# Four graph layers on one Trainium2 core: layer 2's counts on four column tiles of TensorE, and layer 1's last eighth of sources in two pieces

## The chip, the cores and the metric

The kernel runs on one core of a Trainium2 chip. Time is microseconds (us) of device time per execution. The kernel before took 7437.63 us, the median of 10 runs (7422.31 to 7447.1). A profile shows one execution, with these engines: PE (TensorE) does matmuls and PEld its weight loads, DVE is VectorE, ACT is ScalarE, POOL is GpSimd, SP is SyncE, which here only issues DMAs. The granted clock is the share of full speed at which TensorE was allowed to run in a stretch.

## The reference

8192 nodes have 32 features each, and 262,144 edges are sorted by their destination. Four layers follow each other; each adds the sum of its messages to x and normalizes every node's row.

```
out0 = segment_sum(einsum(x[src], weight0[edge_type]), dst)     # 64 relations
out1 = segment_sum(x[src] * edge_weight[:, None], dst)
out2 = segment_sum(x[src], dst)
out3 = segment_sum(messages from x[src], an MLP of edge_attr_32, edge_attr_4, ...)
x = layernorm(x + out_l)                                        # after every layer
```

## The kernel before

A node block is 128 nodes (64 blocks); an edge block g is 1024 edges (256 blocks). All engines' orders are written out by hand in one function: an instruction waits only for the semaphore marks that are named ahead of it (`after`), and each engine works through its list in order. The DMAs of layers 1 and 2 are issued by SP in the order of the program.

**Layer 0** (L878 to L935) is a loop over g from 0 to 257. POOL gathers each edge's row of a table that the prologue (to about 230 us) has made (L454, eight gathers per block, twelve blocks ahead; the two halves of block g+12 wait for marks of PE in block g). DVE cuts the rows into three bf16 parts (L858 to L863) and makes one-hot pairs of the destinations (L583); PE sums eight tiles by destination (L897). Each four blocks the sums are moved out (L869), and as soon as all edges of 8 node blocks are summed, `windows` (L575, shifted sums on PE) and `normalize` (L525 to L537) finish an eighth of x_b, the input of layer 1.

**The matrices.** Blocks 8 to 207 also make 256 matrices of the edges (`matrices`): one-hots on DVE (L638 to L643), products on PE (L654), two evictions on ACT (L658 counts as bytes, L659 weighted sums), and on SP one store of the weighted part to famat (L664) and one of the counts to fcmat (L666). Layer 1 is then a dense product of famat with x_b, layer 2 of fcmat with x_a.

**Layer 1** has 32 destination pieces c (two node blocks each) by 8 source eighths z. One item (c, z) is 1 MB of famat, loaded by SP (L695), and 8 fp32 matmuls with 32 columns of weights (16 records at L717), which go to the four column tiles of PE in turn: four sources sum side by side on 4 x 32 partitions. `take` (ACT, L726) moves a run of items of one c out; `turn_back` (PE, L736) or `turn` (L980) adds the four groups by a matmul with a stack of identities; `add_up` (DVE, L752) adds the run to y1. `plan()` says which item runs in which block g: an item may run once its eighth is normalized and its matrix stored; 1.5 items are due per block, 3 from block 200 on, in at most two runs per block. Of the 256 items, 224 (z = 0 to 6) run in layer 0; the last of them go two per block up to block 245, and blocks 246 to 255 have none. The 32 items of z = 7 follow the last normalization in the *late part* (L990 to L1008): per piece one item, a take, a turn with two matmuls, and a normalization each four pieces. Three 1 MB slots hold items in the loop, six in the late part (`slot_of`). `acc_free` lets the products of a block wait for the adds of the block before.

**Layer 2** (L1013 to L1044) has 16 pieces c of 512 destinations. `bring` (SP, L783) loads 4 MB of counts into one of two buffers; it waits for the last cast of piece c - 2. `widen` casts bytes to bf16 in four ring parts, shared 48, 56 and 24 of 128 between DVE, ACT and POOL (L802, `SHARE`). PE then does 64 matmuls (L1033) with 96 columns of weights (x_a in three bf16 parts, side by side) and 512 of counts, into 96 partitions; ACT moves them out (L1039), `turn` adds the three parts, `normalize` follows each second piece, and SP stores the normalized rows to fxtab (L549).

**Layer 3**, from about 4341 us on, and its self parts (L961, L969) are not touched.

Of the kernel before, what the change touches and what calls it, by code (L numbers as in the profile page):

```python
# [21 lines left out]
P = 128  # L22
N = 8192
E = 262144
D = 32
# [44 lines left out]
RATE = lambda g: 1.5 if g < 200 else 3.0  # L70


def plan():

    normed, n = [], 0
    for g in range(GG):
        if g >= 2 and (g - 2) % 4 == 3:
            while n < NQ1 and ready(n) <= g - 1:
                n += 1
        normed.append(n)  # L80
    got = [0] * NC1
    out, job, due = [], None, 0.0
    for g in range(GG):
        r, m = normed[max(0, g - 1)], made_by(max(0, g - 4))
        due = min(due + RATE(g), 3)
        ended = 0
        while due >= 1:
            if job is None:
                room = NQ1 if ended == 0 else int(due) if ended == 1 else 0
                todo = [(min(r - got[c], room), -c) for c in range(NC1) if m >= 8 * (c + 1) and r > got[c]]  # L90
                if not todo or room == 0:
                    break
                k, c = max(todo)
                job = (-c, got[-c], got[-c] + k)
            c, z0, z1 = job
            z = got[c]
            out.append([g, c, z, z == z0, z + 1 == z1, ended])
            got[c] += 1
            due -= 1
            if z + 1 == z1:  # L100
                job = None
                ended += 1
    if job is not None:
        out[-1][4] = True
    return out
# [46 lines left out]
NQ1 = 8  # L152
# [9 lines left out]
def in_order(ctx: ExitStack, tc, x, a, w0, w1, b1, w2, si, keep):  # L162
# [11 lines left out]
    for k in range(2):  # L174
        m[f"amat{k}"] = dram.tile([NC1 // 2, NQ1, P * 2048 + 2304], FP, name=f"famat{k}")
# [28 lines left out]
def raw_layers(tc, x, a, w0, w1, b1, w2, si, m, bad):  # L204
# [8 lines left out]
    amat = [m["amat0"], m["amat1"]]  # L213
# [44 lines left out]
    st_a = cut(2, 8, 4 * 64).rearrange("p b z (q h w) -> p b z q h w", q=4, h=2)  # L258
# [256 lines left out]
    lnf, lns = m["lnf"], m["lns"]  # L515
# [3 lines left out]
    def normalize(l, c, acc, pm, x_in, x_out, x3=None, more=None):  # L519


        ds = slice(c * LC, (c + 1) * LC)
        y, yc, sq = (lnf[:, k].rearrange("p (d f) -> p d f", f=D) for k in range(3))
# [6 lines left out]
        vm = V.mark(V.e.tensor_sub(yc, y, lns[:, 1, :, None].to_broadcast([P, LC, D])))  # L530
# [6 lines left out]
        ln_last[0] = V.mark(V.e.tensor_tensor(xo, yc, lns[:, 3, :, None].to_broadcast([P, LC, D]), op=OP.mult))  # L537
# [14 lines left out]
    def windows(c, acc, free):  # L552

        d0 = c * LC
        todo = []
        for j in [0, 1, 2, 3, -2, -1, 4]:
            lo, hi = 0, LC
            while 4 * (d0 + lo) + j < 0:
                lo += 1
            while 4 * (d0 + hi - 1) + j >= GG:  # L560
                hi -= 1
            if lo < hi:
                todo.append((j, lo, hi))
# [67 lines left out]
    def matrices(i):  # L631
# [14 lines left out]
        for q in range(4):  # L646
# [4 lines left out]
            for j in range(4):  # L651
                for h in range(2):
# [8 lines left out]
                two[:, :, 256:512].rearrange("p h (z w) -> p h z w", w=32), AF.Copy))  # L661
# [3 lines left out]
                                   st_a[:, b].rearrange("p z q h w -> p z (q h w)")))  # L665
# [8 lines left out]
    m_ld = [Landing(tc, f"ld_m{k}") for k in range(8)]  # L674
    land1, used1, loaded = {}, {}, [0]
    acc_free = [None]
    sums1_free = [None, None]
# [4 lines left out]
    def slot_of(n):  # L682

        r = n - n_in
        if r < 0:
            return 3 + n % 3, n - 3
        order = [0, 1] + [3 + (n_in + k) % 3 for k in range(3)] + [2]
        return order[r % 6], n - 6 if r >= 6 else n - 5 if 2 <= r < 5 else None

    def load1(n, *more):  # L690

        c, z = items[n]
        k, before = slot_of(n)
        S.after(stored[8 * c + 6], stored[8 * c + 7], used1.get(before), *more)
        land1[n] = m_ld[k].add(S.e.dma_start(slot1[k], amat[c // 16][c % 16, z, 0:P * 2048].rearrange("(p w) -> p w", w=2048)))  # L695

    def pump():

        while loaded[0] < n_in + 5:
            n = loaded[0]  # L700
            c, z = items[n]
            before = slot_of(n)[1]
            if made < 8 * (c + 1) or (before is not None and before >= 0 and before not in used1):
                break
# [4 lines left out]
    def products(n, acc, first, last):  # L709

        c, z = items[n]
        k = slot_of(n)[0]
        PE.after(land1[n], normed[z])
        mv = slot1[k].rearrange("p (u h s j) -> p s u h j", h=2, s=8, j=4)
        for s in range(8):
            q = s % 4
            ins = PE.e.matmul(acc[q * D:(q + 1) * D, :].rearrange("p (u h j) -> p u h j", h=2, j=4),  # L717
                              x_b[:, 8 * z + s, :], mv[:, s], start=(first and s < 4), stop=(last and s >= 4),
# [10 lines left out]
    def turn_back():  # L729
# [4 lines left out]
        for c, h, k, am in todo:  # L734
            for d in range(2):
                ins = PE.e.matmul(bank[:, 6, 256 * h + d * D:256 * h + (d + 1) * D], sums1[:, k, d * P:(d + 1) * P], stack,  # L736
# [8 lines left out]
    def add_up():  # L745
# [3 lines left out]
        while added:  # L749
            c, h = added.pop(0)  # L750
            o, v = y1[:, 2 * c:2 * c + 2, :], bank[:, 6, 256 * h:256 * h + 2 * D].rearrange("p (d f) -> p d f", f=D)
# [5 lines left out]
    def layer1(g):  # L757

        ended = []
        while order1 and order1[0][0] == g:  # L760
            _, c, z, first, last, h = order1.pop(0)
            n = n_in - len(order1) - 1
            PE.after(acc_free[0])
            pm = products(n, bank[:, 6, 256 * h:256 * (h + 1)], first, last)
# [3 lines left out]
        for c, h in ended:  # L768
            turned.append((c, h, h, take(sums1[:, h], bank[:, 6, 256 * h:256 * (h + 1)], pm, sums1_free[h])))
# [17 lines left out]
    SHARE = (0, 48, 104, 128)  # L787
# [17 lines left out]
    def early_counts(g):  # L805

        k = g - soon[0]
        if k == 0:
            ring_free[0] = ring_free[1] = now(PE)
            for n in (n_in, n_in + 1):  # L810
# [67 lines left out]
    for g in range(GG + 2):  # L878
        if g >= 2 and (g - 2) % per == per - 1:
            vm = bank_out((g - 2) // per)  # L880
            while done < NB // LC and ready(done) <= g - 1:
                acc = bank[:, (g - 2) // per % 2, 0:LC * D]
                agg_free[(g - 2) // per % 2] = vm = normalize(0, done, acc, windows(done, acc, (vm,)), x_a, x_b)
# [49 lines left out]
    while loaded[0] < min(len(items), n_in + 6):  # L933
# [38 lines left out]
    def turn(l, c, n, am):  # L972

        nb = 2 if l == 1 else 4
        kk = 128 if l == 1 else 96
# [3 lines left out]
        for d in range(nb):  # L979
            ins = PE.e.matmul(bank[:, 2 + o, (d0 + d) * D:(d0 + d + 1) * D], sums[0:kk, n % 2, d * P:(d + 1) * P],  # L980
                              stack[0:kk, :], start=True, stop=True)
        sum_free[n % 2] = pm = PE.mark(ins)
        if d0 + nb == LC:
            out_free[o] = normalize(l, c * nb // LC, bank[:, 2 + o, 0:LC * D], pm, x_b if l == 1 else x_a,
# [8 lines left out]
    for c in range(NC1):  # L993
        b = c % 2
        PE.after(sum_bank[b])
        for e in range(got[c], NQ1):
            pm = products(n, bank[:, b, 0:256], e == got[c], e == NQ1 - 1)
            if n + 6 < len(items):
                load1(n + 6)
            n += 1  # L1000
        sum_bank[b] = am = take(sums[:, b, 0:256], bank[:, b, 0:256], pm, sum_free[b])
        if pend:
            turn(*pend)
        pend = (1, c, c, am)
        if c == 0:
# [8 lines left out]
    for c in range(16):  # L1014
# [14 lines left out]
        for k in range(4):  # L1029
            PE.after(*cast[c][k])  # L1030
            mv = ring[k].rearrange("p (u s j) -> p s u j", s=16, j=4)
            for s in range(16):
                ins = PE.e.matmul(bank[0:96, b, 0:512].rearrange("p (u j) -> p u j", j=4), x3[:, 16 * k + s, :], mv[:, s],  # L1033
                                  start=(k == 0 and s == 0), stop=(k == 3 and s == 15))
# [5 lines left out]
            sums[0:96, b, 0:512].rearrange("p (u j h) -> p u h j", h=2, j=4),  # L1040
            bank[0:96, b, 0:512].rearrange("p (u h j) -> p u h j", h=2, j=4), AF.Copy))
# [158 lines left out]
    for q in range(NQ + LAG3 + 2):  # L1200
# [73 lines left out]
        if 0 <= c < NQ and c % 2 == 1:  # L1274
# [9 lines left out]
            while done < NB // LC and ready(done) <= g + 1:  # L1284
                k, wp = w_bank()
                acc = bank[:, 3 + 2 * k, 0:LC * D]
                windows(done, acc, (w_free[k], gm))
                w_free[k] = normalize(3, done, acc, PE.mark(written(3 + 2 * k, 256)), z, x_a)
# [472 lines left out]
```

## Time and profile before

| stage (us of the span) | length | PE busy | DVE | ACT | POOL | clock | DMA share |
|---|---|---|---|---|---|---|---|
| prologue, 0 to 230 | 230.0 | 160.6 | 72.7 | 121.1 | 70.7 | 0.72 | 0.97 |
| layer 0 with matrices, to 3540 | 3310.0 | 1980.2 | 1893.7 | 1175.4 | 1683.6 | 0.68 to 0.78 | 0.38 to 0.63 |
| rest of layer 0, to 4011.8 | 471.8 | 193.2 | 157.6 | 33.4 | 269.0 | 0.58 | 0.44 |
| late part of layer 1, to 4096.3 | 84.5 | 72.1 | 38.9 | 23.2 | 4.4 | 0.68 | 0.91 |
| layer 2, to 4341.2 | 244.9 | 242.3 | 150.1 | 202.6 | 164.6 | 0.98 | 0.71 |
| layer 3, to 7438.2 | 3097.0 | 2417.6 | 2099.8 | 695.5 | 1937.8 | 0.89 | 0.11 |

The profiled execution took 7439.92 us; its span from the first to the last instruction is 7438.2. Columns of engines are busy us within the stage; records that run together count once. Windows of the trace give such rows for any stretch; timelines list instructions with their start, duration, engine, line, result and operands, and in brackets the idle time before them with what released them ("remote" where the profile knows no releaser). Records of one kind that follow each other are joined (x16 is sixteen records); an fp32 matmul shows as two records.

### The profile page before, as it was taken

What the parts mean: (1) busy time and instruction counts of PE and PEld (TensorE: products, weight loads), DVE (VectorE), ACT (ScalarE), POOL (GpSimd) and SP (SyncE); (2) the same over time, 40 slices, a digit from 0 to 9 for tenths busy, and PEclk for the clock granted to TensorE, in tenths of its full rate; (3) what the DMA queues carried; (4) which work ended last, traced back from release to release, by engine and by line L of the source; (5) the groups of instructions that cost most, each with busy time, mean ns of one, the idle gap of its engine ahead of it and who ended that gap; (6) DMA issues with size and microseconds to landing.
All of it is one profiled execution on the core that took longest, in us unless ns stands there. A gap on an engine that the chain in (4) does not pass through costs nothing.

```text
span 7438.2 us, 89563 instructions
## 1 busy us (share of the span) xinstructions
PE 5066.1 (68%) x34750; PEld 3346.2 (45%) x34750; DVE 4412.9 (59%) x9506; ACT 2251.0 (30%) x3323; POOL 4130.0 (56%) x4236
## 2 busy tenths in 40 slices
PE   7236666666666666666436977887877787877777
PEld 3125555555555555555223534444444444444444
DVE  3246565565566565555324646666666676676666
ACT  5223333333333333333101832222222222222222
POOL 3655555454454454444662666666666666666664
PEclk7557776777777777778556988898989888889988
DMA  9224444544645656667536721110111111111111
GB/s 356 89 57 143 128 140 139 177 145 162 206 155 189 208 187 209 208 214 248 198 113 237 278 88 25 24 25 21 25 24 25 24 24 25 24 25 24 25 24 18
DMA packets 583331, 865.52 MB, mean 116 GB/s; under 512 B 102640, under 2 KB 441840, under 8 KB 549360
## 3 DMA queue, kind: packets, MB, share of 16 engines
q1 hardware_dynamic: 448320, 782.88, 30.3%
q0 software_dynamic: 134144, 73.67, 5.2%
q8 instruction: 276, 4.52, 0.2%
q10 hardware_dynamic: 432, 3.15, 0.1%
q14 instruction: 159, 1.30, 0.1%
HBM read 454.48 MB, written 404.88 MB: 116 GB/s over the span
## 4 chain that ended last, share of the span: by engine, by line
PE 38%; another core or an unknown queue 24%; DVE 19%; ACT 10%; issue 8%; DMA 2%; POOL 1%; SPq 0%; DVEq 0%; ACTq 0%; POOLq 0%
PE bank L654 15%; PE bank L1221 7%; DVE f_arena L1256 4%; PE bank L1211 4%; ACT f_arena L659 3%; PE bank L1033 3%; ACT f_arena L658 3%; DVE f_arena L1252 3%; PE bank L717 2%; DVE f_arena L588 2%; DVE f_arena L1249 1%; ACT bank L1190 1%; PE bank L475 1%; PE bank L897 1%
## 5 line engine op out<-in xcount | busy, mean ns | idle before, releaser
L454 POOL DMA_INDIRECT f_arena<-fytab,f_row x2048 | 1955.3, 955 | 1802.6 <-PE bank L654 813.7
L454 POOL DMA_INDIRECT f_arena<-fxtab,f_src x2048 | 1937.8, 946 | 1112.5 <-issue 562.4
L654 PE MATMUL bank<-f_arena 64*128 64x128 f32 x16384 | 1514.7, 352 | 926.1 <-ACT f_arena L659 554.8
L654 PEld LDWEIGHTS bank<-f_arena 64*128 64x128 f32 x16384 | 1385.7, 257 | 1035.1 <-issue 541.8
L1221 PE MATMUL bank<-f_arena 128*128 128x344 f32 x4096 | 1495.9, 508 | 59.4 <-issue 58.6
L658 ACT ACTIVATE f_arena<-bank 128x512 uint8<-128x512 f32 x1024 | 613.1, 599 | 1796.4 <-remote 834.4
L1221 PEld LDWEIGHTS bank<-f_arena 128*128 128x128 f32 x4096 | 818.8, 211 | 642.4 <-issue 379.3
L1211 PE MATMUL bank<-f_arena 64*128 64x256 f32 x4096 | 660.5, 445 | 552.2 <-ACT bank L1190 456.7
L1190 ACT ACTIVATE bank<-f_arena 128x1024 f32<-128x1024 f32 x512 | 526.2, 1029 | 1118.2 <-DVE f_arena L1256 659.2
L1211 PEld LDWEIGHTS bank<-f_arena 64*128 64x128 f32 x4096 | 391.9, 207 | 942.8 <-ACT bank L1190 585.9
L1249 DVE TENSOR_TENSOR f_arena<-bank,f_arena 128x256 f32<-128x256 f32 x512 | 214.3, 419 | 872.3 <-remote 519.4
L638 DVE TENSOR_TENSOR f_arena<-bank,f_arena 128x1024 f32<-128x1024 bf16 x256 | 312.9, 1222 | 649.1 <-PE bank L654 362.2
L659 ACT ACTIVATE f_arena<-bank 128x512 f32<-128x512 f32 x1024 | 612.0, 598 | 0.0
L640 DVE TENSOR_TENSOR f_arena<-bank,f_arena 128x2048 f32<-128x2048 bf16 x256 | 586.6, 2291 | 8.8
L1256 DVE TENSOR_TENSOR f_arena<-bank,f_arena 128x256 f32<-128x256 f32 x1536 | 551.4, 415 | 0.0
L1177 ACT ACTIVATE f_arena<-bank,f_arena 128x512 f32<-128x512 f32 x256 | 175.5, 686 | 1146.8 <-remote 601.9
L717 PE MATMUL bank<-f_arena,f_x_b 128*32 128x256 f32 x4096 | 377.7, 497 | 74.0 <-issue 29.9
L897 PE MATMUL bank<-f_arena 128*128 128x96 bf16 x2048 | 182.7, 237 | 277.1 <-DVE f_arena L863 133.5
L1252 DVE TENSOR_TENSOR f_arena<-bank,f_arena 128x512 f32<-128x512 f32 x512 | 348.8, 681 | 0.0
L588 DVE TENSOR_TENSOR f_arena<-bank,f_rel 128x512 f32<-128x512 f32 x512 | 348.6, 681 | 0.0
L643 DVE TENSOR_TENSOR f_arena<-f_arena,bank 128x1024 f32<-128x1024 f32 x256 | 309.8, 1210 | 0.0
L752 DVE TENSOR_TENSOR f_arena<-bank,f_arena 128x64 f32<-128x64 f32 x127 | 28.5, 224 | 473.8 <-PE bank L736 354.7
(149 smaller groups left out, 4622.6 us busy)
## 6 DMA issues: line engine op xcount, KB each, us to landing
famat<-f_arena SPq DMA_DIRECT2D x256, 1024.0 KB
f_arena<-famat SPq DMA_DIRECT2D x256, 1024.0 KB, 7.4
fytab<-f_arena SPq DMA_DIRECT2D x64, 1024.0 KB
fcmat<-f_arena SPq DMA_DIRECT2D x256, 256.0 KB
f_arena<-fcmat SPq DMA_DIRECT2D x16, 4096.0 KB, 14.6
f_arena<-fytab,f_row POOLq DMA_INDIRECT x2048
f_arena<-fxtab,f_src POOLq DMA_INDIRECT x2048
f_arena<-laid_ea SPq DMA_DIRECT2D x64, 512.0 KB
```

What stands on the lines that cost most here:

```text
L454: return G.e.indirect_dma_start(out=dest, out_offset=None, in_=table, in_offset=bass.IndirectOffsetOnAxis(ap=ix, axis=0))
L588: return V.e.tensor_tensor(o, iota[:, None, :].to_broadcast([P, n, P]), rel[:, t:t + n, None].to_broadcast([P, n, P]), op=OP.is_equal)
L640: V.e.tensor_tensor(oh_l[:, b], iota2[:, None, :, 0].to_broadcast([P, 16, P]), meta_l[:, pp, k0:k0 + 16, None].to_broadcast([P, 16, P]), o ...
L654: ins = PE.e.matmul(two[:, h].rearrange("p (c s j) -> p c s j", s=64, j=4)[:, :, :, j], oh_l[hs_, b, 4 * q + j, :], oh_k[hs_, b, 4 * q + j ...
L658: A.e.activation(st_c[:, b, q], two[:, :, 0:256], AF.Copy)
L659: pair_free[u] = am = A.mark(A.e.activation(st_a[:, b, :, q].rearrange("p z h w -> p h z w"), two[:, :, 256:512].rearrange("p h (z w) -> p ...
L717: ins = PE.e.matmul(acc[q * D:(q + 1) * D, :].rearrange("p (u h j) -> p u h j", h=2, j=4), x_b[:, 8 * z + s, :], mv[:, s], start=(first an ...
L1190: return A.mark(A.e.activation(wp, b2_s[:, None, :].to_broadcast([P, 4, 256]), AF.Copy))
L1211: ins = PE.e.matmul(wp[:, t, :], hs[hp, q // 2 % 2, c0:c0 + P], w2_s[hp], start=False, stop=True, skip_group_check=True)
L1221: ins = PE.e.matmul(bank[:, g % 2, 0:MW], oh[:, c % NO, t, :], p[:, c % NP, t, :], start=(c % 2 == 0 and t == 0), stop=(c % 2 == 1 and t = ...
L1252: V.e.tensor_tensor(pq[:, :, 0:128].rearrange("p t (o k) -> p t o k", k=16), wp[:, :, 0:128].rearrange("p t (o k) -> p t o k", k=16), a0[: ...
L1256: ins = V.e.tensor_tensor(pq[:, :, 128 + 64 * mm:192 + 64 * mm].rearrange("p t (o i) -> p t o i", i=8), wp[:, :, 192:256].rearrange("p t ( ...
```

## The change

Three things are done. Layer 1's sources are now seven eighths and two pieces of 4 blocks (`SEG`); the first seven eighths and the first half piece (z = 7) run inside layer 0, 256 items in all, and 32 half items (z = 8: 0.5 MB, 4 matmuls, 8 records) are left for the late part. To make room, up to four runs per block are allowed from block 210 (`ROOMS`), with four accumulators; blocks 210 to 215 and 230 to 239 now have 24 matmuls instead of 16, blocks 216 and 240 have 16, blocks 241 to 245 none, and blocks 246 to 253 have four half items each. The last normalization has 4 node blocks. The weighted matrices are stored by two DMAs each (a second array for the last eighth), and the slots are counted in halves, 12 in all. The late part works on pairs of pieces: two half items into one bank, one take of 512 columns, one turn of four matmuls, so 16 of these instead of 32. Layer 2 uses 128x32 weights on four column tiles: 192 matmuls per piece instead of 64, each on a quarter of the array's columns, with sums on 128 partitions; the casts are shared 52, 50 and 26.

```diff
+SEG = [(8 * k, 8) for k in range(7)] + [(56, 4), (60, 4)]
+NQ1 = len(SEG)
+ROOMS = lambda g: 4 if g >= 210 else 2
+
+
+def known(z):
+
+    return min(GG, 4 * (sum(SEG[z]) - 1) + 5)
...
-                room = NQ1 if ended == 0 else int(due) if ended == 1 else 0
+                room = 0 if ended == ROOMS(g) else NQ1 if ended == 0 else int(due)
...
-            due -= 1
+            due -= SEG[z][1] / 8
...
-                                   st_a[:, b].rearrange("p z q h w -> p z (q h w)")))
+                                   st_a[:, b, 0:14].rearrange("p (z f) q h w -> p z (f q h w)", f=2)))
+        st_ld[b].add(S.e.dma_start(last8[i // 8, :, 0:P * 1024].rearrange("z (p w) -> p z w", w=1024)[:, :, P * (i % 8):P * (i % 8 + 1)],
+                                   st_a[:, b, 14:16].rearrange("p z q h w -> p z (q h w)")))
...
+    home, at, user = [], 0, {}
+    for n in range(n_in):
+        k = SEG[items[n][1]][1] // 4
+        at += at % k
+        home.append((6 + at % 6, k, [user.get(6 + (at + e) % 6) for e in range(k)]))
+        for e in range(k):
+            user[6 + (at + e) % 6] = n
+        at += k
+    turns = [0, 1, 2, 3] + [6 + (at + e) % 6 for e in range(6)] + [4, 5]
+    for n in range(n_in, len(items)):
+        k = turns[(n - n_in) % 12]
+        home.append((k, 1, [user.get(k)]))
+        user[k] = n
...
+    acc1 = [bank[:, 6 - 4 * (k // 2), 256 * (k % 2):256 * (k % 2 + 1)] for k in range(4)]
+    sum1 = [sums1[:, 0], sums1[:, 1]] + [late_slot[2][:, 256 * k:256 * (k + 1)] for k in range(2)]
...
+        from_ = amat[c // 16][c % 16, z] if w == 2 else last8[c, z - 7]
+        land1[n] = m_ld[k].add(S.e.dma_start(place(k, w), from_[0:P * 1024 * w].rearrange("(p w) -> p w", w=1024 * w)))
...
-        for s in range(8):
+        mv = place(k, w).rearrange("p (i f v s j) -> p f s i v j", i=8, f=w, v=8, j=4)
+        for s in range(ns):
             q = s % 4
-            ins = PE.e.matmul(acc[q * D:(q + 1) * D, :].rearrange("p (u h j) -> p u h j", h=2, j=4),
-                              x_b[:, 8 * z + s, :], mv[:, s], start=(first and s < 4), stop=(last and s >= 4),
+            ins = PE.e.matmul(acc[q * D:(q + 1) * D, :].rearrange("p (i v j) -> p i v j", v=8, j=4),
+                              x_b[:, s0 + s, :], mv[:, s // 4, q], start=(first and s < 4), stop=(last and s >= ns - 4),
                               tile_position=(0, q * D))
...
+            PE.after(acc_free[0], *(pair_free if h >= 2 else ()))
+            pm = products(n, acc1[h], first, last)
...
+            more = (stored[CB - 1], stored[CB - 2]) if h >= 2 else ()
+            turned.append((c, h, h, take(sum1[h], acc1[h], pm, sums1_free[h], *more)))
...
-    SHARE = (0, 48, 104, 128)
+    SHARE = (0, 52, 102, 128)
...
-    for c in range(NC1):
-        b = c % 2
+    for c2 in range(NC1 // 2):
+        b = c2 % 2
         PE.after(sum_bank[b])
-        for e in range(got[c], NQ1):
-            pm = products(n, bank[:, b, 0:256], e == got[c], e == NQ1 - 1)
-            if n + 6 < len(items):
-                load1(n + 6)
-            n += 1
-        sum_bank[b] = am = take(sums[:, b, 0:256], bank[:, b, 0:256], pm, sum_free[b])
+        for c in (2 * c2, 2 * c2 + 1):
+            for e in range(got[c], NQ1):
+                pm = products(n, bank[:, b, 256 * (c % 2):256 * (c % 2 + 1)], e == got[c], e == NQ1 - 1)
+                if n + 12 < len(items):
+                    load1(n + 12)
+                n += 1
+        sum_bank[b] = am = take(sums[:, b], bank[:, b], pm, sum_free[b])
         if pend:
             turn(*pend)
-        pend = (1, c, c, am)
-        if c == 0:
+        pend = (1, c2, c2, am)
...
-            for s in range(16):
-                ins = PE.e.matmul(bank[0:96, b, 0:512].rearrange("p (u j) -> p u j", j=4), x3[:, 16 * k + s, :], mv[:, s],
-                                  start=(k == 0 and s == 0), stop=(k == 3 and s == 15))
+            for s4 in range(4):
+                for e in range(3):
+                    for q in range(4):
+                        s = 4 * s4 + q
+                        ins = PE.e.matmul(bank[q * D:(q + 1) * D, b, 0:512].rearrange("p (u j) -> p u j", j=4),
+                                          x3[:, 16 * k + s, e * D:(e + 1) * D], mv[:, s],
+                                          start=(k == 0 and s4 == 0 and e == 0), stop=(k == 3 and s4 == 3 and e == 2),
+                                          tile_position=(0, q * D))
...
-            sums[0:96, b, 0:512].rearrange("p (u j h) -> p u h j", h=2, j=4),
-            bank[0:96, b, 0:512].rearrange("p (u h j) -> p u h j", h=2, j=4), AF.Copy))
+            sums[:, b, 0:512].rearrange("p (u j h) -> p u h j", h=2, j=4),
+            bank[:, b, 0:512].rearrange("p (u h j) -> p u h j", h=2, j=4), AF.Copy))
```

`known(z)` takes the place of `ready`: it gives the block from which a piece of sources can be normalized. `normalize` and `windows` take a first node block and their width from the accumulator instead of the number of an eighth; for 8 blocks their instructions are the same.

## The prediction

> **What bounds the kernel now.** I read the table of windows first, then the timelines of PE, ACT, POOL and SyncE where the change acts, then the chain of waits. Layer 3, from 4341 us on, and the first 3540 us hold nothing the change enlarges by much; the stake lies in the 800 us between. Columns: window, its length, busy us (records) of PE, PEld, DVE, ACT and POOL, granted clock, DMA share, GB/s.
>
> ```profile
> 3807.00:3958.70 151.70, 79.05 (x624) 47.78 (x624) 45.67 (x120) 9.01 (x26) 98.03 (x104) 0.61 0.59 199
> 3971.68:4002.50 30.82, 8.44 (x84) 6.43 (x81) 27.82 (x68) 0.00 (x0) 0.00 (x0) 0.52 0.15 60
> 4011.80:4037.90 26.10, 26.09 (x192) 13.60 (x192) 7.65 (x19) 7.26 (x12) 2.93 (x1) 0.50 0.96 374
> 4037.90:4072.00 34.10, 27.97 (x329) 16.24 (x324) 19.58 (x55) 8.91 (x26) 0.00 (x0) 0.95 1.01 413
> 4088.50:4341.20 252.70, 244.24 (x1185) 144.23 (x1181) 154.80 (x135) 206.34 (x105) 166.04 (x61) 0.97 0.71 253
> ```
>
> Row 1, the end of layer 0's loop: POOL paces it. Row 2, the last ten blocks: no products, DVE is full. Rows 3 and 4 are layer 1's late part: PE full at half clock, then nearly full at full clock, DMA near its limit. Row 5, layer 2: PE almost gapless, 13.85 us of L1033 and about 1.2 of L980, L969 and L961 per piece in the chain, 15.07 in all.
>
> **Part 1: eighth 7 moves into the blocks after the last gather.** Its items can start when normalization at g=245 is done; POOL's gathers end at about 3958, so blocks 246 to 253 each get four half items (32 records L717), four takes, four turn-backs, four adds. Each block's products wait for the add of the block before, so this is a chain. Today those blocks cost DVE's 3 us each (L897 every 2.97 us below). The nearest rows are two blocks that had the same 32 records in two items:
>
> ```profile
> 3959.60 1.89 PE L736 MATMUL bank<-f_stack,f_arena 128*128 128x32 f32 x8 [4.82 <-ACT f_arena L726]
> 3962.07 3.64 PE L717 MATMUL bank<-f_arena,f_x_b 128*32 128x256 f32 x32 [0.57 <-DVE f_arena L752]
> 3966.61 1.05 PE L736 MATMUL bank<-f_stack,f_arena 128*128 128x32 f32 x8 [0.21 <-ACT f_arena L726]
> 3968.24 1.93 PE L717 MATMUL bank<-f_arena,f_x_b 128*32 128x256 f32 x32 [0.57 <-DVE f_arena L752]
> 3971.68 1.04 PE L736 MATMUL bank<-f_stack,f_arena 128*128 128x32 f32 x8
> ...
> 3976.40 0.82 PE L897 MATMUL bank<-f_arena 128*128 128x96 bf16 x8 [3.67 <-DVE f_arena L863]
> 3979.37 0.82 PE L897 MATMUL bank<-f_arena 128*128 128x96 bf16 x8 [2.15 <-DVE f_arena L863]
> ```
>
> From turn-back to turn-back: 3966.61 - 3959.60 = 7.01 us at half clock, 5.07 at full. Four items instead of two add two takes (0.69 for two in L726's row), eight records L736 (1.89 cold, 1.04 warm) and two adds (224 ns each in the page's group L752): about +2.9 cold, +2.1 warm, so 9.9 or 7.2. The stretch showed 0.58 mean clock; I take 8.9. Eight blocks at 8.9 and 3 for the last give 74, where g=246 to 255 take 30.8 today (row 2): **+43** (+30 warm, +52 cold). Beside it: DVE's 3 us per block runs in PE's products, no longer seen.
>
> The last normalization has 4 blocks instead of 8: 28 records L575 took 5.68 us, about 18 remain, -2.
>
> **Part 2: the late items halve.** Today per piece 16 records L717 and 4 of L980:
>
> ```profile
> 4016.37 1.94 PE L717 MATMUL bank<-f_arena,f_x_b 128*32 128x256 f32 x16
> 4018.24 1.06 PE L980 MATMUL bank<-f_stack,f_arena 128*128 128x32 f32 x4
> 4019.23 1.94 PE L717 MATMUL bank<-f_arena,f_x_b 128*32 128x256 f32 x16
> ```
>
> 4019.23 - 4016.37 = 2.86 us cold; 32 pieces took 76.7 with the warm stretch. Afterwards a pair has 16 L717 (1.87) and 8 L980 (1.9): 3.77 cold, about 2.0 warm; 16 pairs are 60 to 33. Late loads shrink from 32 MB to 16, so DMA no longer limits. The first 20 us are cold today with no gap on PE; I take 58: **-19** (bounds -14, -44).
>
> The Trainium skill, "TensorE: Matmul & The Clock Gate", Part 1, has the full clock follow some 3.4 us of sustained activity. Row 3 disagrees: 26.09 us busy of 26.10 at 0.50. By the page the late part would be 33 us and the drain all warm, and my sum would fall by 38.
>
> **Part 3: the loop before.** Blocks 230 to 239 now run three items (48 records L717) instead of two. Today POOL's eight gathers take about 10 us and then it waits:
>
> ```profile
> 3816.12 0.94 POOL L454 DMA_INDIRECT f_arena<-fytab,f_row  x1 [0.30 <-issue]
> 3819.02 0.94 POOL L454 DMA_INDIRECT f_arena<-fytab,f_row  x1 [1.95 <-remote]
> ```
>
> That wait (a block takes 11.65 us in all) is for PE's mark, behind turn-back and products; the trace names no releaser. No row shows a third item there: it costs between 0 (hidden in POOL's 10 us) and 2.3 (16 records L717 cold, 1.94, and a take, 0.35). I take 1.15, the middle, as no row is nearer to one end: 10 blocks, **+12** (0 to +23). Blocks 210 to 215 likewise get a third item, but before the late loads crowd in: +3 (0 to +14). Blocks 241 to 245 lose all products, and with them the 1.95 wait at most: **-7** (-4 to -10). Each matrix is now stored by two DMAs, with 1152 descriptors instead of 1024 and one more issue on SP's queue, ahead of fcmat's store and of layer 1's loads. Nothing waits closely for these, since L654 and ACT's L658 and L659 stand in the chain of waits there and SP doesn't. Should SP's queue fall behind, 200 blocks at 0.05 would be +10; I take **+3**. The new waits cost nothing: the third and fourth products of a block wait for L659 of the last matrix, their takes for its stores, both over by block 208.
>
> **Part 4: layer 2 on four column tiles.** Do four tiles run at once? The page's groups say so of L717 (columns: busy us, mean ns of one, idle before):
>
> ```profile
> L717 PE MATMUL bank<-f_arena,f_x_b 128*32 128x256 f32 x4096 | 377.7, 497 | 74.0 <-issue 29.9
> ```
>
> 4096 records of 497 ns one after the other would be 2036 us; they kept PE busy for 377.7, so more than four overlap on average. I take the same for bf16, which no row shows. Today L1033's 64 matmuls take 13.85 us, 0.2164 each. Afterwards there are 192 of the same 512 columns; four at once, they cost 48 x 0.2164 = 10.4, and with the 1.2 of the others 11.6. But PE isn't alone near 15:
>
> ```profile
> 4242.27 0.36 SPq L549 DMA_DIRECT2D fxtab<-f_x_b  x1
> 4242.73 11.67 SPq L783 DMA_DIRECT2D f_arena<-fcmat  x2
> ```
>
> and on ACT
>
> ```profile
> 4253.88 0.63 ACT L1039 ACTIVATE f_arena<-bank 96x512 f32<-96x512 f32 x1
> 4254.40 0.25 ACT L963 ACTIVATE f_arena<-bank 128x128 f32<-128x128 f32 x1
> 4257.20 6.27 ACT L802 ACTIVATE f_arena<-f_arena 128x3584 bf16<-128x3584 uint8 x2 [2.56 <-DMA f_arena<-fcmat]
> ```
>
> SP issues a count load behind the store of normalized rows (4242.27), and the casts wait for its landing at 4257.18, 14.5 us later. Every second load stands so: with ACT's four casts of 3.13 before it and 3.3 us from the last of them (4239.4) to the issue, that is 30.3 us for two pieces: 15.1 each, PE's own period. ACT's casts shrink by 50/56 (3.13 to 2.8), POOL's grow by 26/24. If this chain holds, only the ends and the casts' share are won; if not, ACT sets (4 x 2.8 + 0.63 + 0.25 + half of 0.7) = 12.4 us, 2.6 less for 15 pieces, -39. Nothing gained is the other end. I take **-11**, near the transfer row.
>
> The same page, Part 3, measured three column tiles at 2.38 times. Four in proportion are 3.17, an estimate: 13.1 us, still under the chain; the sum stays.
>
> **Sum.** +43 -2 -19 +12 +3 -7 +3 -11 = +22. The profiled execution took 7439.92, 2.3 above the median of 7437.63: 7462 against 7440, and 7459 against the median.
>
> **Rivals.** 0.2% (15 us) is about what a measurement here can tell from no change.
> (a) *Full clock after the gathers* (faster). If PE keeps the 1.00 it had at 4038 to 4072, the drain is +30 and the late part -44 instead of +43 and -19: -16 against before, 7422; it decides from about half of today's half-clock time running full. For it: that stretch and 0.97 throughout layer 2. Against it: row 3, gapless at 0.50, and row 2's 0.52.
> (b) *Layer 2 released* (near nothing). Neither load nor cast binds, 12.4 us a piece: 22 - 28 = -6, 7432. For it: DMA share 0.71 there is below the 1.01 of row 4. Against it: the 14.5 us landing. With (a) together, about 7395.
> (c) *Four bf16 tiles do not overlap as the fp32 ones do.* Two at once would be 96 x 0.2164 + 1.2 = 22 us a piece: +105 over before, 7550. For it: no bf16 tile appears in the trace. Against it: L717.
> (d) *The terms cancel*: a mixed clock in the drain (+36), the third items hidden in POOL's time (0 instead of +15), the rest as above: 22 - 7 - 15 = 0, 7438.
>
> **How the numbers follow.** The forecast (slower: the chain in the drain, 7459) has 0.45, (c) 0.03; (b) alone and (d) together 0.27; (a) 0.17, (a) with (b) 0.08. So slower 0.48, same 0.27, faster 0.25. The range, 7408 to 7494, goes down to (a) with half of (b), and up to the cold drain (+9), a full price of the third items (+22) and layer 2 at nothing (+11), less the 7 that hardly coincide; it leaves out (c), (a) with all of (b), and all upper bounds at once.
>
> **What would show it.** Right: L736 to L736 about 9 us in the last blocks, last L575 some 43 us later after the last gather than today's 44; late part near 58 us with 0.5 clock; 15 us between count loads with idle PE in layer 2. Wrong: blocks of 6 us or less, a period under 13 us in layer 2, L717 no slower per block at 230 to 239, or L1033 records at 0.2 us each in a row.

## The result, and the profile after

The changed kernel takes 7475.65 us (median of 8 runs, 7460.9 to 7484.34); the kernel before, run beside it, 7431.93. The ratio is 1.0058, with a 95% interval of 1.0049 to 1.0067: slower by 0.58%, some 44 us. The profiled execution took 7463.25 (span 7461.5), 12 us under its median, where that of before was 8 over the median it is now compared with. So the two traces differ by 23 us, and 20 us of the difference of medians can't be assigned from this pair.

| stretch | before | after | difference | forecast |
|---|---|---|---|---|
| to block 8 (code not touched) | 441.5 | 445.9 | +4.5 | 0 |
| block 8 to 207, matrices | 3074.1 | 3082.9 | +8.8 | +3 |
| block 207 to the last gather | 440.6 | 441.9 | +1.3 | +8 |
| last gather to block 246 | 15.2 | 14.0 | -1.2 | 0 |
| block 246 to the late part | 40.5 | 77.2 | +36.7 | +41 |
| late part of layer 1 | 84.5 | 59.7 | -24.8 | -19 |
| layer 2 | 244.9 | 250.5 | +5.6 | -11 |
| layer 3 (not touched) | 3097.0 | 3089.4 | -7.6 | 0 |

Windows of the changed kernel's trace for the last three touched stages (window, length, busy us and records of PE, PEld, DVE, ACT, POOL, granted clock, DMA share, GB/s):

```profile
3984.70:4061.90 77.20, 54.83 (x482) 36.07 (x482) 36.96 (x106) 10.71 (x34) 0.00 (x0) 0.68 0.64 218
4061.90:4121.70 59.80, 50.65 (x388) 32.87 (x392) 39.15 (x107) 20.41 (x34) 4.75 (x2) 0.61 0.65 247
4121.70:4372.20 250.50, 224.29 (x3219) 134.69 (x3220) 190.37 (x122) 182.35 (x102) 157.00 (x60) 0.93 0.69 244
```

Before, DVE held the last ten blocks (28 of 31 us busy, the second row of the prediction); now PE has 55 of 77 us there, and DVE is idle half of them. In layer 2 PE is no longer gapless: 26 us of the 250 are idle.

PE's timeline in the last blocks shows the chain, block by block:

```profile
3998.70 1.94 PE L760 MATMUL bank<-f_stack,f_arena 128*128 128x32 f32 x16 [0.72 <-ACT f_arena L750]
4001.73 3.35 PE L741 MATMUL bank<-f_arena,f_x_b 128*32 128x256 f32 x32 [1.09 <-DVE f_arena L776]
4005.30 0.51 PE L923 MATMUL bank<-f_arena 128*128 128x96 bf16 x8 [0.21 <-DVE f_arena L888]
4006.58 2.23 PE L760 MATMUL bank<-f_stack,f_arena 128*128 128x32 f32 x16 [0.77 <-ACT f_arena L750]
4009.90 3.64 PE L741 MATMUL bank<-f_arena,f_x_b 128*32 128x256 f32 x32 [1.09 <-DVE f_arena L776]
```

Turn-back (L760), wait for the adds (L776), products (L741), the block's own sums (L923), wait for the takes (L750), turn-back: 4006.58 - 3998.70 = 7.9 us, where blocks were 2.97 us apart before. Of the 7.9, PE works 5.8 (1.94, 3.35 and 0.51) and waits 2.1, so the chain is made of PE's own work more than of its waits.

In layer 2, SP's queue and ACT show what takes PE's place:

```profile
4205.17 0.36 SPq L559 DMA_DIRECT2D fxtab<-f_x_b  x1
4205.62 10.46 SPq L808 DMA_DIRECT2D f_arena<-fcmat  x2
4238.83 0.36 SPq L559 DMA_DIRECT2D fxtab<-f_x_b  x1
4239.28 0.53 SPq L808 DMA_DIRECT2D f_arena<-fcmat  x1
```

```profile
4220.93 11.16 ACT L827 ACTIVATE f_arena<-f_arena 128x3200 bf16<-128x3200 uint8 x4 [4.55 <-DMA f_arena<-fcmat]
4231.99 0.66 ACT L1070 ACTIVATE f_arena<-bank 128x512 f32<-128x512 f32 x1
4235.61 0.42 ACT L542 ACTIVATE f_lnf<-f_lnf 128x256 f32<-128x256 f32 x1 [2.96 <-DVE f_lnf L540]
```

A load of counts is issued right behind a store of normalized rows, at 4205.62 and again at 4239.28: two pieces in 33.66 us, 16.8 each, where it was 30.13 before (from the 4242.73 of the prediction's row to this one):

```profile
4272.86 0.53 SPq L783 DMA_DIRECT2D f_arena<-fcmat  x1
```

From issue to the first cast are 15.3 us, the four casts are 11.16, and from the last cast (4232.09) to the next issue 7.2. Before, these were 14.5, 12.4 and 3.3. Why the last one grew shows at DVE, with its last casts and the normalization's first and last instruction, before and then after:

```profile
4235.71 1.81 DVE L802 CAST f_arena<-f_arena 128x3072 bf16<-128x3072 uint8 x1 [1.12 <-PE bank L1033]
4237.45 0.41 DVE L525 TENSOR_TENSOR f_lnf<-bank,x_a 128x256 f32<-128x256 f32 x1
4241.27 0.97 DVE L537 TENSOR_TENSOR f_x_b<-f_lnf,f_lns 128x256 f32<-128x256 f32 x1
```

```profile
4220.93 11.43 DVE L827 CAST f_arena<-f_arena 128x3328 bf16<-128x3328 uint8 x4 [5.44 <-DMA f_arena<-fcmat]
4232.28 0.41 DVE L535 TENSOR_TENSOR f_lnf<-bank,x_a 128x256 f32<-128x256 f32 x1
4237.09 1.72 DVE L547 TENSOR_TENSOR f_x_b<-f_lnf,f_lns 128x256 f32<-128x256 f32 x1
```

Before, DVE ended its casts 1.9 us ahead of ACT, and the normalization took 4.8 us (to 4242.24, then the store). After, DVE ends them 0.3 us behind ACT, and the normalization takes 6.5 us.

### The profile page after: what moved, and what is told of

Read it like the earlier page. It is cut to its first block, busy times and chain, and to the rows that moved or that the text cites. A ratio compares the mean times of both kernels' runs of the same rounds, so it can differ in the third digit from the quotient of the medians.

```text
span 7461.5 us, 94280 instructions
## 1 busy us (share of the span) xinstructions
PE 5044.3 (68%) x36932; PEld 3352.8 (45%) x36932; DVE 4462.6 (60%) x9545; ACT 2237.9 (30%) x3341; POOL 4123.8 (55%) x4236
## 4 chain that ended last, share of the span: by engine, by line
PE 36%; another core or an unknown queue 21%; DVE 20%; ACT 9%; issue 9%; DMA 4%; POOL 1%; SPq 0%; DVEq 0%; ACTq 0%; POOLq 0%
PE bank L664 15%; PE bank L1252 7%; PE bank L1242 4%; DVE f_arena L1287 4%; ACT f_arena L669 3%; ACT f_arena L668 3%; PE bank L741 3%; DVE f_arena L1283 3%; DVE f_arena L598 2%; DVE f_arena L1280 1%; DMA f_arena<-fcmat 1%; ACT bank L1221 1%; PE bank L923 1%; PE bank L483 1%
## 5 line engine op out<-in xcount | busy, mean ns | idle before, releaser
L664 PE MATMUL bank<-f_arena 64*128 64x128 f32 x16384 | 1517.7, 353 | 950.4 <-ACT f_arena L669 533.8
L664 PEld LDWEIGHTS bank<-f_arena 64*128 64x128 f32 x16384 | 1388.9, 258 | 1056.7 <-issue 551.5
L741 PE MATMUL bank<-f_arena,f_x_b 128*32 128x256 f32 x4096 | 370.6, 504 | 76.4 <-DVE f_arena L776 35.4
L923 PE MATMUL bank<-f_arena 128*128 128x96 bf16 x2048 | 183.3, 237 | 320.3 <-DVE f_arena L888 206.5
L923 PEld LDWEIGHTS bank<-f_arena 128*128 128x128 bf16 x2048 | 123.9, 113 | 422.5 <-DVE f_arena L888 220.0
## 6 DMA issues: line engine op xcount, KB each, us to landing
f_arena<-fcmat SPq DMA_DIRECT2D x16, 4096.0 KB, 15.2
```

The lines of the kernel that those rows point to most:

```text
L664: ins = PE.e.matmul(two[:, h].rearrange("p (c s j) -> p c s j", s=64, j=4)[:, :, :, j], oh_l[hs_, b, 4 * q + j, :], oh_k[hs_, b, 4 * q + j ...
L741: ins = PE.e.matmul(acc[q * D:(q + 1) * D, :].rearrange("p (i v j) -> p i v j", v=8, j=4), x_b[:, s0 + s, :], mv[:, s // 4, q], start=(fir ...
```

## The experiments

The first four ran on one chip, on which the kernel before takes 7445.43 us, like the pair above (7418 to 7447). The other eight ran on chips on which the same kernel takes 5777 to 5787 us; what differs there is told at `change_again`. Ratios are always to the kernel before on the same chip.

**`l2_old`**: layer 1 as changed, layer 2 as before.

```diff
-            for s4 in range(4):
-                for e in range(3):
-                    for q in range(4):
...
+            for s in range(16):
+                ins = PE.e.matmul(bank[0:96, b, 0:512].rearrange("p (u j) -> p u j", j=4), x3[:, 16 * k + s, :], mv[:, s],
+                                  start=(k == 0 and s == 0), stop=(k == 3 and s == 15))
...
-    SHARE = (0, 52, 102, 128)
+    SHARE = (0, 48, 104, 128)
```

> The changed kernel with layer 2 as before (64 matmuls of 96 columns, 96 partitions, shares 48/56/24); layer 1 stays changed. Theory: layer 2 is held by the chain load, casts, normalization, store, next load, and tiling only moved its period from 15.07 to 16.8 us a piece; then layer 2 takes 245 us again instead of 250.5, and the time is 7470 (5 to 6 us under the changed kernel). Rival: tiling is a gain or loss of PE's own, larger than that: over 15 us either way (below 7460 or above 7490).

Measured: 7495.27, ratio 1.0064 (1.0041 to 1.0087), which the whole change's 1.0058 can't be told from. Layer 2 took 244.3 us. So tiling cost layer 2 some 6 us, as expected, and the slowdown sits in layer 1's part. The 7470 itself was missed: this chip is slower by 13 us with the kernel before, and 12 us over are left, which the interval (17 us either way) doesn't tell from nothing.

**`l2_only`**: layer 1 as before; of the change's diff only the hunks at L1033, L1039, SHARE and the full 128 partitions in `turn`.

> The kernel before with layer 2 tiled and shared as in the change; layer 1 as before. Theory (loads hold layer 2): 5 to 6 us slower than before, 7437. Rival (the tiles pay, and only layer 1's new end, which runs into layer 2's first loads, hides it): 30 us faster, about 7400.

Measured: 7455.1, ratio 1.0012 (1.0003 to 1.0022), +9 us. Layer 2 took 250.2 us, as in the change; the rival falls. Its pieces start 13.7, 12.9 and 12.7 us apart until normalizations and stores set in; then come one distance of 21.3 and three of 13.3 to 14.5, and from there on 16 to 17.6.

**`l2_late_store`**: the same, with the store behind the load on SP.

```diff
         if l == 2:
-            S.after(ln_last[0])
-            x_st.add(S.e.dma_start(xtab.rearrange("(d p) f -> p d f", p=P)[:, ds, :], xo))
+            held.append((ln_last[0], ds, xo))
...
         bring(c + 2)
+        put()      # waits for the mark and stores what was held
         widen(c + 1)
```

> As the one with only layer 2 tiled, but SP issues the store of the normalized rows after the next count load and no longer before it. Theory: a load no longer stands behind the normalization (5.9 us from the last cast to the load's issue in the changed kernel), a buffer's round is 15.2 of landing and 11.2 of casts, so 13.2 us per piece, where PE's own 13.2 (11.8 and 1.4 of turns) is about as long: layer 2 takes 215 to 225 us, 20 to 30 less than before, 7402 to 7412. Rival (DMA's rate or the casts themselves hold it): period still over 15.5, 7430 or more.

Measured: 7423.71, ratio 0.9973 (0.9963 to 0.9983): 21.7 us faster than before, and 31 faster than with the tiles alone. Layer 2 took 223.4 us. By the ratios this version beats both kernels. PE is close to gapless again, at 13.3 us per piece:

```profile
4183.71 11.95 PE L1045 MATMUL bank<-f_arena 128*32 128x512 bf16 x192
4195.59 1.08 PE L989 MATMUL bank<-f_stack,f_arena 128*128 128x32 f32 x8
4196.50 0.47 PE L978 MATMUL bank<-f_arena 128*128 128x128 f32 x2
4196.80 0.27 PE L970 MATMUL bank<-f_ident,f_x_b 128*128 128x128 f32 x1
4197.01 11.92 PE L1045 MATMUL bank<-f_arena 128*32 128x512 bf16 x192
```

and SP's store (L558) now starts after the load, off the way:

```profile
4187.46 14.66 SPq L792 DMA_DIRECT2D f_arena<-fcmat  x2
4204.23 2.06 SPq L558 DMA_DIRECT2D fxtab<-f_x_b  x1
4215.56 14.56 SPq L792 DMA_DIRECT2D f_arena<-fcmat  x2
```

**`no_drain`**: the change, with z = 7's half items in the late part instead of the last blocks.

```diff
-            while n < NQ1 and known(n) <= g - 1:
+            while n < 7 and known(n) <= g - 1:
                 n += 1
```

> The changed kernel with the 32 half items of z = 7 moved from the blocks after the last gather to the late part (64 half items there). Theory: the stretch from block 246 to the late part falls from 77 to about 40 us (-37); the late part gets 16 more records per pair, 1.0 us at full clock to 1.9 at half, +16 to +30, so 7455 to 7468. Rival (the loss sits in the loop before, by third items and the split stores, and the chain of the last blocks is hidden): the stretch stays above 60 us, and the time rises by the late items to 7485 or more.

Measured: 7468.3, ratio 1.0032 (1.0022 to 1.0042). The stretch from block 246 fell from 77.2 to 36.1 us, and the late part rose from 59.7 to 83.2:

```profile
4006.60:4042.70 36.10, 12.39 (x102) 10.03 (x102) 29.13 (x75) 0.61 (x2) 0.00 (x0) 0.50 0.00 0
4042.70:4125.90 83.20, 65.99 (x640) 34.14 (x640) 40.27 (x107) 21.36 (x34) 4.76 (x2) 0.77 0.96 375
```

So moving the half items ahead bought 23.5 us in the late part for 41 us in the last blocks. By the ratios the move costs 0.26%, 19 us, of the whole 0.58%; by the stretches it is 17.6 (27 against `l2_old`, which has the changed layer 1, ran on this same chip and took 82.2 and 64.0 us there). The rival falls for this part, but 0.32% is left, of which layer 2 explains 6 to 9 us. In both kernels of this chip with split stores, the matrix blocks took longer than in the two without:

| block 8 to 207, one chip | us |
|---|---|
| `l2_only` / `l2_late_store`, one store per matrix | 3071.7 / 3066.7 |
| `l2_old` / `no_drain`, two stores, one with short runs | 3109.9 / 3104.0 |

These are single executions: those of `l2_old` and `no_drain` took 13 us more than their medians, those of the other two 3 more and 2 less, and the changed kernel's in the table of the result 12 less. If such a distance is laid on this stretch alone, all three kernels with two stores come to 22 to 29 us over those with one. That is an estimate; the traces don't show where the distance lies, and layer 3, which is not touched, differs by 7.6 us between the two traces of the result.

**`two_stores`**, **`two_stores_again`** and **`two_stores_third`**: the same kernel three times, `l2_late_store` with each weighted matrix stored by two DMAs in the old layout.

```diff
-        st_ld[b].add(S.e.dma_start(amat[i // 128][i // 8 % 16, :, 0:P * 2048]...
+        for z_ in (slice(0, 7), slice(7, 8)):
+            st_ld[b].add(S.e.dma_start(amat[i // 128][i // 8 % 16, z_, 0:P * 2048]...
```

> The kernel before with layer 2 tiled and the late store of rows (7423.7 us, 21.7 below its kernel before), and each weighted matrix stored by two DMAs (seven eighths, one eighth) into the old layout: the same 1024 runs of 1 KB, one more issue. In the kernels with the split store the stretch from block 8 to block 207 took 3083 to 3110 us, without it 3067 to 3074. Theory 1 (one more transfer in SP's queue and in what ACT's next eviction waits for): that stretch gets about 30 us longer, 7450. Theory 2 (the short runs and their DMA time): nothing, 7424.

> The kernel before with layer 2 tiled, the late store of rows, and each weighted matrix stored by two DMAs into the old layout, once more, to be set beside the other kernel of this call, which has one store. Where PE paces the matrix blocks (the kernel before takes about 7440 us): theory 1 (the extra transfer): block 8 to 207 takes 20 to 35 us longer than in the kernel with one store, ratio to before about 1.001. Theory 2 (only the short runs or the eviction into 16-element runs cost): the stretch is equal within 8 us, ratio about 0.997. Where DVE paces them (5787 us): equal.

> The kernel before with layer 2 tiled, the late store of rows, and two stores per matrix in the old layout, beside the changed kernel on one chip. Where the kernel before takes about 7440 us: theory 1 (the extra transfer and issue): block 8 to 207 as long as in the changed kernel (within 8 us), ratio about 1.001. Theory 2 (short runs or the eviction): 20 us or more shorter than in the changed kernel, ratio about 0.997. Where it takes about 5780 us: as it was measured twice, 0.996.

Measured: ratios 0.9956 (0.994 to 0.9973), 0.9964 (0.9951 to 0.9976) and 0.9952 (0.9935 to 0.9968). All fell on chips of the 5780 us sort, where the question could only be asked in part. There block 8 to 207 took 2044.5 us in the second run, beside 2032.3 in `late_store_only` on the same chip, and 2054.0 in the third, beside 2055.4 in the changed kernel on another: the extra transfer alone is as long as the change's split, within 1.4 us, and 12 us longer than one store. But the same kernel differs by 9.5 us between these two chips, and the 12 us hardly reach the end: from block 8 to the last gather are 2449 and 2453 us in the first pair, 2450 in both of the second. Part of the 12 us can be seen at ACT, whose first eviction into a buffer waits for the landing of what was stored from it. ACT's waits over that stretch, in `late_store_only` and then in `two_stores_again` (waiting line, releaser, us in all, times, longest):

```profile
ACT f_arena L667 <- DMA fcmat<-f_arena: 122.7, 34, 10.5
```

```profile
ACT f_arena L667 <- DMA fcmat<-f_arena: 132.2, 40, 10.3
```

On the other sort of chip, the wait of this eviction for a releaser the trace doesn't name is 812 and 850 us with one store and 886 and 916 with two on the chip of the table (834 and 845 in the pair of the result). The 32 to 43 us there (22 to 28 by the estimate above) fit theory 1, but no run with the extra transfer alone fell on such a chip: whether transfer, short runs or the eviction's shape sets them stays open.

**`short_runs`**: `l2_late_store` with one store per matrix as before, but all in runs of 512 bytes; loads come in 4 KB pieces to match. The kernel leaves out the reordering that this needs, so its layer 1 sums are not the reference's.

```diff
-        st_ld[b].add(S.e.dma_start(amat[i // 128][i // 8 % 16, :, 0:P * 2048]...
+        st_ld[b].add(S.e.dma_start(amat[i // 128][i // 8 % 16].rearrange("z (t y) -> (z t) y", t=2)[:, 0:P * 1024]...
```

> The same kernel with one store per matrix, but all of it in runs of 512 bytes (2048 instead of 1024; the change has 1152); each item's elements then lie in another order in its slot, so layer 1's sums are not the reference's. Theory 2 (short runs): eight times the change's extra runs, the stretch from block 8 to 207 over 60 us longer, 7485 or more. Theory 1 (the extra transfer): under 10 us longer, about 7430.

Measured (three executions, on the chip of the first `two_stores`): 5813.75, ratio 1.0044 (1.0028 to 1.006). Block 8 to 207 took 2117.4 us, against 2053 to 2059 in the three other kernels profiled on that chip, which have two stores per matrix and 1024 or 1152 runs. Short runs do cost, some 60 us for 1024 more per matrix; the change's 128 more, an eighth, would be 7 to 8 us by proportion, though `two_stores_third` and the changed kernel differ by less.

**`two_chained`** and **`two_unchained`**: two half items per block in blocks 246 to 255, on two pairs of accumulators; the second waits only for its own pair's add.

```diff
-ROOMS = lambda g: 4 if g >= 210 else 2
+ROOMS = lambda g: 4 if 210 <= g < 246 else 2
...
-            PE.after(acc_free[0], *(pair_free if h >= 2 else ()))
+            PE.after(acc_free[h // 2], *(pair_free if h >= 2 else ()))     # two_unchained
```

> The changed kernel with two half items per block in blocks 246 to 255 (20 in all, 12 more in the late part), on two pairs of accumulators by turns, but still waiting for the last add before the next products. If the work on PE and ACT sets a block's time there, half the items take half of 8.1 us: 4.1, as DVE allows at 3.0. If the chain of waits does, a block takes 5 to 6 us.

> The same, but products wait only for the add of their own pair of accumulators, two blocks back. If the chain of waits sets the time, a block falls to 4 us or less, some 15 us less in all than with the wait; if the work does, nothing changes between the two (within 4 us).

Measured: 5771.13, ratio 0.9972 (0.9961 to 0.9983), and 5777.01, 0.9977 (0.9967 to 0.9987). Inconclusive: on this chip the blocks come some 10 us apart in both, since POOL's gathers pace them, so neither work nor chain is seen. The chain of the changed kernel thus rests on its timeline above and on `no_drain`.

**`late_store_only`**: layer 2 untiled, only the store put behind the load, by the edit shown at `l2_late_store`.

> The kernel before with layer 2 untiled and only the store of the rows issued behind the next count load. Theory: untiled, PE's 15.07 us per piece is a limit of its own, as long as the chain through the load; freeing the load then changes nothing: layer 2 245 us, the time within 5 us of before. Rival: the load alone set the 15.07 us; then layer 2 falls to 225 us and the time by 20, with or without tiles.

Measured: 5775.33, ratio 0.9999 (0.9989 to 1.0008); layer 2 took 244.2 us, its pieces 15.1 apart as before:

```profile
2911.40:3155.60 244.20, 241.64 (x1172) 142.16 (x1173) 142.18 (x122) 205.13 (x102) 164.66 (x60) 0.98 0.72 253
```

PE is busy 241.6 of 244.2. So PE and the chain through the load were two limits of nearly equal length. Removing the chain alone is worth nothing, tiling alone +5 to +9 us, both together -22.

**`change_again`**: the changed kernel on a chip of the other sort.

> The changed kernel itself once more. Where the kernel before takes about 7440 us, POOL waits for PE's marks in layer 0 and the last blocks run after the last gather: ratio 1.006 again, 75 to 82 us from block 246 to the late part, 3080 to 3110 us from block 8 to 207. Where it takes about 5780 us, POOL's gathers never wait for PE (blocks 246 to 255 come 10 us apart, as fast as POOL gathers), so the products of z = 7 lie beside gathers: theory (the chain costs only what is not covered): the stretch is no longer than without them (98 to 100 us), the late part is 20 us shorter, and the changed kernel is 5 to 20 us faster than before. Rival (products in the last blocks cost their 8 us each anywhere): 15 us or more slower.

Measured: 5763.32, ratio 0.9963 (0.9949 to 0.9977): there the change is faster by 0.37%. The windows from block 246 to the late part, the late part and layer 2, first of this kernel, then of `late_store_only` (whose layer 1 is that of before; it ran on another chip of this sort):

```profile
2721.90:2820.30 98.40, 63.73 (x486) 43.92 (x489) 37.65 (x107) 10.71 (x34) 65.14 (x69) 0.57 0.56 183
2820.30:2885.90 65.60, 59.37 (x388) 38.25 (x391) 39.01 (x107) 20.68 (x34) 4.75 (x2) 0.50 0.63 224
2885.90:3136.00 250.10, 223.11 (x3219) 135.15 (x3220) 192.48 (x122) 182.26 (x102) 155.62 (x60) 0.92 0.69 245
```

```profile
2721.40:2821.30 99.90, 14.73 (x120) 12.40 (x116) 31.19 (x76) 1.41 (x4) 64.31 (x69) 0.53 0.13 31
2821.30:2911.40 90.10, 82.04 (x640) 44.62 (x640) 38.92 (x107) 23.46 (x50) 4.40 (x2) 0.58 0.86 340
```

POOL is busy in the first stretch (65 us of gathers), where it did nothing in the pair above. PE did 49 us more work there in no more time, because the products lay between gathers. The late part is 24.5 us shorter and layer 2 again 6 longer, which is the 18 us. (The matrix blocks are 23 us longer here too, but the last gather starts at 2806.9 us against 2805.5: POOL paces all that comes before it.) The reason is in POOL's waits. POOL's gathers of layer 0 in the changed kernel, on the page of the result's run and then of `change_again`:

```profile
L462 POOL DMA_INDIRECT f_arena<-fytab,f_row x2048 | 1956.7, 955 | 1815.3 <-PE bank L664 746.0
```

```profile
L462 POOL DMA_INDIRECT f_arena<-fytab,f_row x2048 | 1959.3, 957 | 652.2 <-issue 544.2
```

One gather takes the same time, 955 and 957 ns, but on the first sort of chip POOL stood 1815 us, 746 of them for the matrices' products (L664) alone; on the second 652, of which 544 are its own issue gaps. So on the second sort POOL sets the pace and gathers until 5 us before block 255's sums (2811.9); on the first it waits for PE through the loop and starts its last gather 15 us before block 246, with the last blocks' rows in hand.

## Why the prediction was right or wrong

The side was right and the range, 7408 to 7494, held 7475.65; the forecast of 7459 gave half the slowdown. That the two traces differ by 23 us and the forecast said 22 is luck: layer 2 (16.6) and the matrix blocks (5.8) lie 22 us over their terms, and the other stretches 21 under theirs (third items 6.7, last gather 1.2, last blocks 4.3, late part 5.8, untouched code 3.1).

**Right: the chain of the last blocks.** The forecast of 8.9 us per block (+43, and -2 for the smaller normalization) met 7.7 to 8.8 and +36.7; `no_drain` gave 41 for the chain alone, on its chip. The mechanism was the one described: products wait for the adds of the block before, with DVE's own work beside them. Its condition, that no gather runs any more, was read from the trace of before and holds for that sort of chip alone; I had not said that the sign hangs on it.

**Right in the main: the late part.** 58 us were forecast for what took 76.7 before, and some 54 were measured (4061.9 to 4115.6, the end of the last turn); with the tail up to layer 2 it is 59.7 against 84.5, 6 us better than the term. The clock there was 0.61, on the cold side that I had taken, but in another order: full from 4065.5 on, and half from 4080, when PE had no more gaps.

```profile
4065.50:4080.00 14.50, 11.63 (x133) 8.24 (x129) 8.45 (x24) 6.63 (x11) 0.00 (x0) 0.97 1.03 398
4080.00:4113.60 33.60, 33.49 (x217) 21.43 (x216) 22.20 (x63) 8.89 (x19) 1.57 (x1) 0.50 0.39 150
```

Rival (a), a full clock after the gathers, fell, with 0.68 in the last blocks and this 0.61. The Trainium skill, "TensorE: Matmul & The Clock Gate", Part 1, would have the clock full after some 3.4 us of sustained activity. Two windows speak against it here: 0.50 with PE busy 33.49 of 33.60 us, and in `change_again` 0.50 with PE busy 59.37 of 65.60.

**Wrong: layer 2, the step "I take -11, near the transfer row".** The chain was found (load behind the store, 14.5 us landing, casts, 3.3 us to the next issue), and rival (b), layer 2 released, fell as the forecast had it. But its terms were held as they stood in a schedule that PE paced. With PE out of the way the 3.3 us became 7.2: the normalization, which the store waits for, stands in DVE's queue behind four casts, which now end 2.1 us later beside ACT's, and it took 6.5 us instead of 4.8. The landing became 15.3. The gain of 1.2 in the casts was used up several times over: +5.6 to +9 instead of -11. `l2_late_store` is the proof, 27 us off layer 2 by an order of two DMAs. As for the price of a tile, 192 matmuls took 11.8 to 12 us where nothing held them, not 10.4: 13.85 / 11.8 is 1.17, and for three times as many matmuls that is 3.5 at once, not four. The same page's Part 3 has 2.38 for three column tiles; the 3.17 estimated from it for four was low, as 10.4 was optimistic. The prediction's L717 row couldn't settle this: 2036 / 377.7 is 5.4, more than the four tiles there are, so its 497 ns are not the time that one record holds its tile.

**Mis-sized: the stores, +3.** "Nothing waits closely for these" was wrong. ACT's next eviction into a buffer waits until what was stored from it has landed; I had read the wait of L658 as PE's alone. No run shows the 0.05 us per block from which the term was taken. The matrix blocks took 8.8 us more in the pair of traces and 32 to 43 on the chip of the first experiments, 22 to 29 in all three by the estimate given with their table; where POOL paces the loop, 12 in one pair were down to 5 by the last gather. With such a size the medians' 44 us come out (26, for instance, and +1.3, -1.2, +36.7, -24.8 and +5.6 make 43.6), but the traces don't show it, and the runs don't divide this term into its causes on the chips of the result.

**Mis-sized, small: the third items.** I took +15 -7; block 207 to the last gather came to +1.3. In the terms of the working, the lower bound (hidden in POOL's ten us) held.

**Slips that don't move the forecast.** The late part's bound of -14 is -16 by its own rows (60.3 - 76.7). Rival (c), 105 us over before, is 7543 and not 7550, and with the other terms of the sum 7575.

## What to carry to other kernels

When two limits of a stage are nearly equal, making one engine faster can let the other's chain stretch (here from 30.13 to 33.66 us for two pieces), since work that the slow engine had spaced now meets in the queues: follow the freed chain through every in-order queue (here SP's, and DVE's behind it) before pricing the gain, and free both together. Work moved into a stretch is free only under cover; name the cover, and ask whether it stands on every chip. A store out of a buffer can be on the path of whoever fills that buffer next.

## What the runs showed of the hardware

Chips of one kind differ: the same kernel takes 7418 to 7462 us on some and 5774 to 5795 on others, and the same change is 0.58% slower and 0.37% faster. What the traces show is waits for PE that end late while POOL issues gathers on the first sort. There DVE waited for the sums of the normalization at block 245 until POOL's last gather had ended (3971.7), though PE's last record of them ended at 3959.1. That PE's marks reach the other engines late then is a reading of this, which no run isolates. Both of the following rows are DVE's first instruction of that normalization, in the changed kernel and in `change_again`:

```profile
3976.03 0.29 DVE L535 TENSOR_TENSOR f_lnf<-bank,x_a 128x128 f32<-128x128 f32 x1 [20.64 <-remote]
```

```profile
2706.16 0.29 DVE L535 TENSOR_TENSOR f_lnf<-bank,x_a 128x128 f32<-128x128 f32 x1 [3.84 <-PE bank L585]
```

Why the two sorts differ, no run here tells.
